# Window attention, MLP and dynamic convolution on one core: parameters folded inside the first rounds, softmax sums moved ahead, the taps' small network along the free axis

## The chip, the cores and the metric

The kernel runs on one core of a Trainium2 chip, in fp32. The metric is the device time of one execution in microseconds (us); lower is better. A core has five engines that work side by side (in the kernel before TensorE is busy for 95% of the span, VectorE for 66%, ScalarE for 51%, GpSimd for 21%), each on its own list of instructions: TensorE (matmul, "PE"), VectorE ("DVE"), ScalarE ("ACT"), GpSimd ("POOL") and SyncE ("SP", used here to issue DMA transfers). What stands in front of an instruction in that list can hold it up: below, copies stand behind a table load of 1.28 us and two convolution starts of 1.96 us together, and with these moved behind them (`a_tableys`) TensorE's 78.2 us of waits for copies are gone.

## The reference, cut to what matters

Layer 0 is a Swin block (window attention with shift, then an MLP), layer 1 a masked 3x3 depthwise convolution whose weights come from a small network on the pooled image.

```python
# x: (16, 192, 56, 56); 7x7 windows, 6 heads
h   = layernorm(x over channels) * g1 + b1            # rolled by -3, cut into windows
q, k, v = split(h @ qkv_w + qkv_b)                    # q scaled
p   = softmax(q @ k.T + rel_bias + mask)
x1  = x + unroll(p @ v @ proj_w + proj_b)
y   = x1 + gelu(layernorm(x1) * g2 + b2 @ fc1_w + fc1_b) @ fc2_w + fc2_b
t   = relu(batchnorm(mean(y over pixels) @ w1.T))     # 48 numbers per image
wt  = t @ w2.T + b2                                   # taps per channel and image, 4 of 9 used
out = depthwise_conv3x3(y, wt) + bias
```

## The kernel before

An image is cut into four strips, 64 in all; a strip is 7 rows of the upper half of the image and the 7 rows 28 below them. A **round** `i` does the MLP of strip `i-2` and the attention of strip `i` side by side, scales strip `i+1`, and takes statistics of strips `i+2` and `i-1`. The layer norms' gains and shifts are folded into the weights once, ahead of all rounds. The finished image is convolved in six **pieces**, one begun in the MLP's gap (`between`) and, when two more are ready, two begun on ScalarE ahead of the softmax copies.

```python
    images = {0: load_x(0, nc.sync)}          # the whole image, 1.48 MB
    # ... all parameters loaded (ScalarE's queue), folded on VectorE and TensorE ...

    def attention_scores(i, q4, q2):
        def add(wp):      # scores on TensorE, then e = scores + bias on VectorE
            ...
        def top(wp):      # maximum, subtraction (VectorE), Exp (ScalarE)
            ...
        def share(wp):    # sum, reciprocal (VectorE), product into prob (GpSimd)
            ...
        add(0)
        add(1)
        top(0)
        add(2)
        top(1)
        add(3)
        top(2)
        share(0)
        top(3)
        for wp in range(1, 4):
            share(wp)

    def attention_turn(i, wp):                # transposes of prob; two PSUM buffers
        pt = banks(f"pt_{i}_{wp}", wp % 2)
        ...                                   # six transposes
        prt = one.tile([128, 2, 3 * PW], F32, tag="prt", name=f"prt_{i}_{wp}", bufs=4)
        nc.scalar.copy(prt, pt[:, :, : 3 * PW])
        return prt

    def taps_second(b, tt):
        pw = bank(f"w_{b}", 1)
        for kc in range(2):
            for t in range(NTAP):
                c = kc * NTAP + t
                mm(pw[:, c : c + 1], w2t[:, kc, t, :], tt, True, True)
        ...

    for i in range(-2, NS + 2):
        keys = {}
        ...                                   # statistics (TensorE) of strips i+2 and i-1
        dev = norm_devs(keys) if keys else None       # square, Sqrt (ScalarE), reciprocal (VectorE)
        if has(i + 1):
            norm1_scale(i + 1, dvs.pop(0))
        if keys:
            dvs.update(norm_spread(keys, dev))        # deviation spread over partitions by DMA
        ...
            hid = one.tile([128, NFC, 2, T], F32, tag="hid", name=f"hid_{i - 2}")
            mlp_first(i - 2, yns.pop(i - 2), hid, between)
        ...
            table(AF.Exp)
            attention_scores(i, *qs.pop(i))
        table(AF.Sqrt)                        # loads the square root's table on ScalarE
        ys = [(*c, conv_begin(*c)) for c in conv_ready(2)]
        ...                                   # MLP second part on TensorE; a turn after each share of it
        o = attention_values(i, prts) if has(i) else None
        for c in ys:
            conv_rest(*c)
        if has(i + 1):
            qs[i + 1] = attention_qk(i + 1)
        ...                                   # taps_second, project, values of strip i+1
```

## Time and profile before

| | before |
|---|---|
| time, median of 3 executions | 3442.24 us (3442.2 to 3443.28) |
| TensorE busy | 3270.0 us, 95% |
| first scores / first MLP matmul | 98.95 / 190.45 us |
| steady cycle of four rounds (one image) | 205.44 us |

The lines that carry the bound are in the prediction. Where the texts say cold, TensorE ran at the slower pace of the start: a statistics matmul took 0.86 us at 58 us and 0.49 at 98. A row of a timeline gives the start, the duration from first to last, the engine, the source line, the operation with its tiles, the number of instructions joined in the row, and in brackets how long the engine had been idle and who ended that. Three more readings of the kernel before: the taps' matmuls (first rows), and the two deviations at the start. The second square (72.04) waits for the DMA that spreads the first deviation, as both use one tile.

```profile
61.13 0.49 ACT L382 ACTIVATE dev<-st 64x392 f32<-64x392 f32 x1 [20.51 <-PE st L89]
...
72.04 0.49 ACT L382 ACTIVATE dev<-st 64x392 f32<-64x392 f32 x1 [6.15 <-DMA dv<-dev]
...
1017.69 0.34 PE L89 MATMUL t<-pooled,w1t 128*48 128x1 f32 x4
...
1049.18 1.84 PE L89 MATMUL w<-tt,w2t 48*128 48x1 f32 x16
1050.95 1.41 PE L89 MATMUL pp<-o,wp 128*64 128x392 f32 x5
```

The groups of instructions give busy time and the mean in ns. The softmax's subtraction has a mean of 906 ns since the fourth of each round runs beside GpSimd's product (1.31 us at 1084.08, against 0.77 for each of the three before it).

```profile
L577 DVE TENSOR_TENSOR e<-e,top 113x588 f32<-113x588 f32 x256 | 231.9, 906 | 8.9
```

### The profile page before, as it was taken

How to read it: one execution, taken by the hardware profiler on the slowest of the kernel's cores; microseconds unless marked ns; L12 is line 12 of the kernel's file. 1: busy time of each engine (PE TensorE's matmuls, PEld its weight loads, DVE VectorE, ACT ScalarE, POOL GpSimd, SP SyncE). 2: the span in 40 equal slices, each digit the busy share in tenths (PEclk: the TensorE clock that was granted, in tenths of full speed). 3: DMA queues.
4: the chain of work that ended last, by engine and by line, in shares of the span. 5: the costliest groups of instructions: out<-in, count | busy, mean ns of one | idle time of the engine just before them, and what ended most of it. 6: DMA issues, size and time to landing. Idle time of an engine off the chain costs nothing.

```text
span 3441.8 us, 65409 instructions
## 1 busy us (share of the span) xinstructions
PE 3270.0 (95%) x26902; PEld 1937.9 (56%) x26902; DVE 2259.6 (66%) x4098; ACT 1765.9 (51%) x2884; POOL 734.6 (21%) x606
## 2 busy tenths in 40 slices
PE   4599999999999999999999999999999999999996
PEld 2455555556555555555555555555655555555553
DVE  2655576675766667576675866667576775857664
ACT  1454555555555555455555555555455555555553
POOL 1112212212212212212212212212221221221210
PEclk9799999999999999999999999999999999999998
DMA  2100111010110201111120110201112020111001
GB/s 68 43 20 11 48 39 48 25 56 25 42 54 25 62 24 35 47 39 50 31 62 13 46 48 28 58 24 39 44 38 55 26 62 18 40 48 33 26 19 53
DMA packets 83085, 135.34 MB, mean 39 GB/s; under 512 B 25537, under 2 KB 65890, under 8 KB 80738
## 3 DMA queue, kind: packets, MB, share of 16 engines
q1 hardware_dynamic: 76304, 128.65, 13.1%
q8 instruction: 212, 3.47, 0.4%
q10 hardware_dynamic: 6482, 2.51, 0.3%
q14 instruction: 87, 0.71, 0.1%
HBM read 41.15 MB, written 38.54 MB: 23 GB/s over the span
## 4 chain that ended last, share of the span: by engine, by line
PE 71%; DVE 18%; ACT 4%; issue 4%; POOL 1%; DMA 0%; ACTq 0%; SPq 0%; DVEq 0%; POOLq 0%
PE ph L89 24%; PE pv L89 8%; PE pp L89 7%; PE po L89 6%; DVE e L570 5%; PE st L89 5%; DVE top L576 5%; PE pk L89 4%; PE pf L89 4%; DVE e L577 4%; PE pq L89 4%; PE pe L89 4%; PE pt L607 3%; DVE tot L584 2%; ACT y L762 2%
## 5 line engine op out<-in xcount | busy, mean ns | idle before, releaser
L586 POOL TENSOR_TENSOR prob<-e,tot 113x588 f32<-113x588 f32 x256 | 295.3, 1175 | 2561.2 <-DVE tot L585 2561.2
L89 PE MATMUL ph<-yn,wf 128*128 128x392 f32 (+1 forms) x3072 | 819.2, 508 | 1.1 <-ACT hid L679 1.1
L89 PE MATMUL pf<-hid,wf 128*64 128x392 f32 (+1 forms) x3072 | 818.3, 497 | 0.0
L89 PEld LDWEIGHTS ph<-yn,wf 128*128 128x128 f32 (+1 forms) x3072 | 409.8, 187 | 401.8 <-ACT hid L679 85.0
L89 PEld LDWEIGHTS pf<-hid,wf 128*64 128x64 f32 (+1 forms) x3072 | 376.6, 163 | 310.7 <-issue 121.1
L679 ACT ACTIVATE hid<-ph,f1b 128x784 f32<-128x784 f32 x384 | 337.3, 914 | 216.6 <-PE ph L89 216.3
L477 DVE TENSOR_SCALAR kbd<-pk,qkb 32x784 f32<-32x784 f32 x256 | 263.7, 1030 | 281.0 <-PE pk L89 278.2
L580 ACT ACTIVATE e<-e 113x588 f32<-113x588 f32 x256 | 177.5, 693 | 420.6 <-DVE e L577 420.6
L777 DVE SCALAR_TENSOR_TENSOR y<-x,wt,y 128x770 f32<-128x770 f32 x288 | 342.6, 1199 | 23.8 <-ACT y L762 17.0
L570 DVE TENSOR_TENSOR e<-sc,bias_t 113x588 f32<-113x588 f32 x256 | 190.3, 764 | 226.5 <-PE sc L89 226.4
L89 PE MATMUL pv<-wqkv,win 64*128 64x192 f32 (+1 forms) x2048 | 275.8, 330 | 3.1 <-DVE kbd L477 3.1
L89 PEld LDWEIGHTS pv<-wqkv,win 64*128 64x128 f32 (+1 forms) x2048 | 253.7, 190 | 36.1 <-issue 18.3
L540 DVE COPY vbd<-pv 49x192 f32<-49x192 f32 x512 | 159.8, 350 | 173.0 <-PE pv L89 88.2
L607 PE MATMUL pt<-ident,prob 113*128 113x113 f32 x1536 | 199.0, 267 | 76.7 <-POOL prob L586 65.4
L607 PEld LDWEIGHTS pt<-ident,prob 113*128 113x128 f32 x1536 | 162.4, 143 | 190.6 <-POOL prob L586 159.1
L345 ACT ACT_TABLE_LOAD x199 | 255.3, 1283 | 3.5
L89 PE MATMUL pp<-o,wp 128*128 128x392 f32 (+2 forms) x896 | 250.7, 521 | 0.5 <-ACT o L639 0.5
L613 ACT COPY prt<-pt 128x678 f32<-128x678 f32 x256 | 180.9, 717 | 136.6 <-PE pt L607 136.5
L577 DVE TENSOR_TENSOR e<-e,top 113x588 f32<-113x588 f32 x256 | 231.9, 906 | 8.9
L724 DVE SCALAR_TENSOR_TENSOR x<-pf,f2b,x 128x784 f32<-128x784 f32 x64 | 66.2, 1034 | 230.6 <-PE pf L89 230.6
L542 ACT COPY vbd<-pv 49x192 f32<-49x192 f32 x512 | 135.4, 312 | 147.3 <-DVE vbd L540 147.3
L474 ACT ACTIVATE q<-pq,qkb 128x784 f32<-128x784 f32 x64 | 58.6, 916 | 290.3 <-PE pq L89 290.3
(114 smaller groups left out, 4236.6 us busy)
## 6 DMA issues: line engine op xcount, KB each, us to landing
dv<-dev SPq DMA_DIRECT2D x1024, 49.0 KB
x<-in_x_dram SPq DMA_DIRECT2D x16, 1484.0 KB
out_dram<-y SPq DMA_DIRECT2D x48, 392.0 KB
out_dram<-y SPq DMA_DIRECT2D x48, 196.0 KB
x<-in_x_dram SPq DMA_DIRECT2D x16, 392.0 KB
x<-in_x_dram SPq DMA_DIRECT2D x16, 350.0 KB
out_dram<-y SPq DMA_DIRECT2D x16, 308.0 KB
out_dram<-y SPq DMA_DIRECT2D x16, 154.0 KB
```

The costliest lines, as they stand in the source:

```text
L89: nc.tensor.matmul(dst, lhs, rhs, start=start, stop=stop, skip_group_check=True)
L345: nc.scalar.activation(junk, eps_t[0:1], func)
L477: nc.vector.tensor_scalar(kbd[p, 0:2, :, h % 2, :], pk[p, :, :T].rearrange("p h (w t) -> p h w t", t=N), qkb[p, 1:2], None, ALU.add,)
L570: nc.vector.tensor_tensor(e, sc[:PW, :, : HEADS * N], rel, ALU.add)
L576: nc.vector.tensor_reduce(t, ehs[wp], AX.X, ALU.max)
L577: nc.vector.tensor_tensor(ehs[wp], ehs[wp], t.broadcast_to([PW, 2 * HEADS, N]), ALU.subtract)
L580: nc.scalar.activation(es[wp], es[wp], AF.Exp)
L586: nc.gpsimd.tensor_tensor(prob[wp][:PW, :, 0:N], ehs[wp], t.broadcast_to([PW, 2 * HEADS, N]), ALU.mult)
L607: nc.tensor.transpose(pt[:, a, g * PW : (g + 1) * PW], prob[wp][:PW, h : h + 2, :].rearrange("p h k -> p (h k)"), ident[:PW, :PW],)
L613: nc.scalar.copy(prt, pt[:, :, : 3 * PW])
L679: nc.scalar.activation(hid[:, f], phs[f][:, :, :T], AF.Gelu, bias=f1b[:, f : f + 1])
L777: nc.vector.scalar_tensor_tensor(dst, src, wt[:, kc, t : t + 1], dst, ALU.mult, ALU.add)
```

## The change

Three parts. (1) Start: only what strip 0 needs is loaded first, strip by strip; the other parameters come on GpSimd's queue and are folded inside rounds 0 and 1, which get an order of their own. (2) Taps: the small network lies along the free axis, two matmuls and five VectorE instructions instead of 2 + 8 matmuls (each shows as two records in the trace: x4 and x16 above). (3) Softmax order: sums go ahead, so that GpSimd's product of one group no longer falls on the next subtraction and comes in time for the transposes. The diff, cut:

```diff
-        add(0)
-        add(1)
-        top(0)
-        add(2)
-        top(1)
-        add(3)
-        top(2)
-        share(0)
-        top(3)
-        for wp in range(1, 4):
-            share(wp)
+        if between is None:
+            add(0)
+            top(0)
+            add(1)
+            top(1)
+            share(0)
+            add(2)
+            top(2)
+            share(1)
+            add(3)
+            top(3)
+            share(2)
+        else:
+            ...                               # rounds 0 and 1: additions first
+        share(3)
...
-    def taps_first(b, pooled):
+    def taps(b, pooled):
         pt = bank(f"t_{b}", 1)
         for kc in range(2):
-            mm(pt[:RED, 0:1], w1t[:, kc, :], pooled[:, kc, :], kc == 0, kc == 1)
...
-                mm(pw[:, c : c + 1], w2t[:, kc, t, :], tt, True, True)
+            mm(pt[:, 0:RED], pooled[:, kc].broadcast_to([128, 128]), w1t[:, kc], kc == 0, kc == 1)
...
+    load_rows(*images[0], 0, 0, WS, nc.sync)              # strip 0: 7 rows of each half
+    nc.scalar.dma_start(raw[:, 0], qkv_w[0:C0])
...
+    load_rows(*images[0], 0, WS, 2 * WS, nc.sync)
+    load_rows(*images[0], 0, 2 * WS, HALF, nc.sync)
+    nc.sync.dma_start(mask_t, win_mask)
...                                                        # + 14 bias loads on the same queue
+    norm_squares("1_0", 0, 0, nc.gpsimd)
+    fold_scale(raw, g1, eff)
+    keys = stats_of(-2)
+    pm = fold_means(eff, 3 * DIM, "fq", 0)
+    dvs.update(norm_spread(keys, norm_devs(keys), (nc.sync, nc.scalar)))
+    norm_squares("1_1", 1, 0, nc.gpsimd)
+    fold_center(eff, 3 * DIM, pm)
...                                                        # wqkv, then the bias matmuls
+    keys = stats_of(-1)
+    dev = norm_devs(keys)
+    norm1_scale(0, dvs.pop(0), nc.vector)
...
+    for i, extra in ((0, (proj_bias, mlp_weights)), (1, (taps_weights,))):
+        attention_scores(
+            i, *qs.pop(i), lambda: norm1_scale(i + 1, dvs.pop(0), nc.gpsimd)
+        )
+        qs[i + 1] = attention_qk(i + 1)
+        for e in extra:
+            e()
+        keys = stats_of(i)
+        dev = norm_devs(keys)
...
```

## The prediction

> **What bounds the kernel now.** I read first the page's busy shares with its slices, then TensorE's waits from 200 to 3400 us, then the timelines of one steady round, and last those of the first 190 us.
>
> ```profile
> PE 3270.0 (95%) x26902; PEld 1937.9 (56%) x26902; DVE 2259.6 (66%) x4098; ACT 1765.9 (51%) x2884; POOL 734.6 (21%) x606
> ...
> PE   4599999999999999999999999999999999999996
> ...
> PEclk9799999999999999999999999999999999999998
> ```
>
> TensorE is full from the third slice to the last but one; only the first two slices (172 us) and the tail are thin. So in the middle a part matters only if it removes TensorE's work or one of its waits. TensorE's waits from 200 to 3400 us (total, times, longest) sum to 61.9 us, and nearly all are these two:
>
> ```profile
> PE pt L607 <- POOL prob L586: 47.5, 62, 0.8
> PE pt L607 <- ACT prt L613: 11.2, 29, 0.4
> ```
>
> 62 rounds wait 0.77 us once for GpSimd's softmax product. The second wait comes in the rounds in which ScalarE begins two convolution pieces ahead of its copies. One such round, TensorE, ScalarE and VectorE in turn:
>
> ```profile
> 1087.72 0.80 PE L607 MATMUL pt<-ident,prob 113*128 113x113 f32 x6 [0.77 <-POOL prob L586]
> 1088.36 1.50 PE L89 MATMUL pf<-hid,wf 128*128 128x392 f32 x4
> 1090.24 0.77 PE L607 MATMUL pt<-ident,prob 113*128 113x113 f32 x6 [0.39 <-ACT prt L613]
> ...
> 1085.42 0.69 ACT L580 ACTIVATE e<-e 113x588 f32<-113x588 f32 x1 [2.21 <-DVE e L577]
> 1086.13 1.28 ACT L345 ACT_TABLE_LOAD   x1
> ...
> 1087.54 1.96 ACT L762 ACTIVATE y<-x,cb,wt 128x784 f32<-128x784 f32 x2
> 1089.40 1.32 ACT L613 COPY prt<-pt 128x678 f32<-128x678 f32 x2
> ...
> 1084.08 1.31 DVE L577 TENSOR_TENSOR e<-e,top 113x588 f32<-113x588 f32 x1
> ```
>
> The second transpose (1087.72) waits for its probabilities; the third reuses the first one's PSUM bank and waits for its copy. That copy stands behind the fourth exponential, a table load and two convolution starts. The fourth exponential starts as VectorE's fourth subtraction ends, so that subtraction sets the third transpose.
>
> The start, TensorE's timeline:
>
> ```profile
> 79.25 2.98 PE L89 MATMUL pk<-win,wqkv 128*128 128x392 f32 x4 [14.14 <-DVE win L423]
> ...
> 98.95 1.23 PE L89 MATMUL sc<-kbd,q 64*64 64x98 f32 x48
> ...
> 145.41 1.74 PE L89 MATMUL sc<-kbd,q 64*64 64x98 f32 x72
> ...
> 190.45 4.75 PE L89 MATMUL ph<-yn,wf 128*128 128x392 f32 x14
> ```
>
> All weights are folded by 58 us; only then come the first statistics (58.2), the first projection (79), rounds 0 and 1 (about 45 us each), and the first MLP at 190.45. From there on TensorE is full.
>
> [...] a statistics matmul takes 0.86 us at 58 us and 0.49 at 98; but folding kept TensorE busy from 35 to 48 us without warming it. [...] 16 tap matmuls with 128-column weights advance 1.77 us, 111 ns each. [...] the fourth subtraction takes 1.31 us beside GpSimd's product, the others 0.77. [...] the 144 KB halves of the weights landed about 2.8 us after issue, and eight spreads of one deviation, issued in turn, took 6.5 us (65.5 to 72.0).
>
> **Part 1, the start.** I walk the new order with durations of the old trace.
> - Statistics of strip 0 need only its 600 KB, now loaded first. The first image's 1.48 MB transfer was in by 7.9 us, so the strip should be in by about 5.5. Squares on GpSimd 2.3, statistics (cold) until about 10, deviation chain as before (square 0.5, table load 1.28 which now lies on it, root 0.6, reciprocal 2.6) until about 15.
> - The spread goes half through the sync queue, behind 14 strips, the mask and 14 bias loads at about 0.6 us each, so it is issued at 17 to 20 and lands at 22 to 25. The second deviation reuses the tile, so it starts then: 5.1 us, then scaling; the first projection starts 2.8 us after the reciprocal, at about 31.
> - Projection to the end of the key copy 11.0 us, value part 9.8 (both from 79.25 to 100.05). The attention-bias sums (5.57 us) fit the 5.97 us in which VectorE waited there. First scores S0 at about 52 instead of 98.95.
> - Round 0 gets longer. VectorE: four additions, tops and shares to S0+13.3, keys to 17.5. Then the projection bias (about 3), first MLP weights scaled (0.5), their means on TensorE (about 4.5 cold), 24 bias matmuls (0.26 each cold as in 5.72 us for 22; here about 5), statistics 2, to about S0+33. Then deviation, transposes, values, projection and value part: second scores at S0+51. Before: 46.5.
> - Round 1: 9.6 us of softmax, keys 4.2; meanwhile eleven parameter loads on GpSimd's queue[...] land about 28 us in and stand before the deviation chain on ScalarE and VectorE. Reciprocal at 33.5, values and projection to 46, statistics 2.7: first MLP 49 us after the scores. Before: 45.0.
> - Sum: 52 + 51 + 49 = 152 instead of 190.45: **38.5 us gained**, about 47 by the early start less 8.5 given back.
>
> **Part 2, taps.** An image's taps cost TensorE 0.27 us (1017.69 to 1017.96) and 1.77 us (1049.18 to 1050.95) of advance. Now two matmuls, in four passes of 128 weight columns, about 0.5 us. 1.54 us by 15 images in the full stretch: **23 us gained**. VectorE gets five small instructions, about 1.5 us, in a gap of 5.5 us before the scores. The last image's taps shorten the tail by about 0.6.
>
> **Part 3, softmax order.** From the first addition, pitches are 0.69 for an addition (0.79 where its reduction follows directly), 1.48 for maximum and subtraction, 0.93 for sum and reciprocal. Old: the fourth subtraction ends after four additions, four tops with the slow subtraction, one share: 10.2 us, as seen. New: 4 x 0.79 + 4 x 1.48 + 2 x 0.93 = 10.9. The slow subtraction goes, but two shares and four bubbles stand before the end.
> - The second product is ready at 8.7 + 1.2 = 9.9 us, and TensorE comes at 11.7: the 0.77 us wait goes.
> - The fourth exponential starts 0.74 later, and so does the first copy. Third transpose without pieces: possible at 13.9, TensorE there at 13.7: wait 0.25. With pieces: possible at 15.0 + 0.74 = 15.7: wait 2.0 where both waits were 1.16.
> - 32 rounds gain 0.52, 30 lose 0.74 to 0.84: **about 6 us lost**.
>
> **Sum:** 3442.2 - 38.5 - 23 - 0.6 + 6 = 3386 us, 1.6% less.
>
> **Rivals.**
> - *The softmax order wins outright:* the 47.5 us go and nothing replaces them. For it: that wait is the largest. Against: ScalarE's copy already makes 29 waits of 0.39. If that did not move, 47 more would go: 3333.
> - *The start overlaps better:* the folding fills waits in which TensorE would idle anyway, and rounds 0 and 1 keep 45 us each: 47 gained, 3377. Against: bias matmuls stand before the statistics in TensorE's order, and the parameters before the deviation in VectorE's.
> - *GpSimd's queue becomes the bound of the start:* 16 loads before it scales strip 1, and 11 between its last product and the MLP input. [...] The page has no GpSimd load to size this by.
> - *The taps' saving is not real* since a broadcast operand loads slowly: 15 us less, 3401.
>
> **Range and chances.** Start 28 to 52 gained, taps 12 to 26, order from 12 lost to 25 gained: errors are independent, so some 30 us about the sum; 3352 to 3414. 2% less is about 3373, 13 below the middle: 0.29 faster, 0.70 same, 0.01 slower.
>
> **What would show it right or wrong.** The first scores at about 52 us and the first MLP matmul at about 152; waits of transposes for products gone, waits for copies grown to 50 to 70 us, about 2 us each with pieces; the tap matmuls down to four records of about 0.5 us an image; no slow fourth subtraction. I am wrong by most if the copy waits stay as they are, or if the first MLP stands far from 152.

## The result, and the profile after

| | before | after |
|---|---|---|
| time, median | 3442.22 us (3440.63 to 3443.28) | 3416.48 us (3415.19 to 3417.38) |
| ratio | | 0.9925, 95% interval 0.9908 to 0.9943 |
| first projection / first scores | 79.25 / 98.95 us | 41.22 / 61.86 us |
| second scores / first MLP matmul | 145.41 / 190.45 us | 119.79 / 172.73 us |
| cycle of four rounds | 205.44 us | 204.75 us |

The kernel before has one execution more here than in the first table. Here and below a ratio is the mean time of one kernel's fast executions over that of the other's in the same rounds, so not quite the ratio of the medians quoted. The gain is 0.75%, about 26 us where 56 were predicted, and the time lies 2.5 us above the range.

The page after: TensorE has 28.5 us less work and is as full as before.

```profile
PE 3241.5 (95%) x26642; PEld 1917.0 (56%) x26642; DVE 2256.0 (66%) x4143; ACT 1755.0 (51%) x2863; POOL 745.6 (22%) x656
...
PE   4799999999999999999999999999999999999996
...
PEclk8799999999999999999999999999999999999998
```

TensorE's waits from 200 to 3400 us (total us, times, longest): GpSimd's 47.5 us are gone and ScalarE's copies cost 78.2 us instead of 11.2.

```profile
PE pt L500 <- ACT prt L506: 78.2, 62, 2.6
```

The timeline after. In the round with two pieces ScalarE runs the table load (1065.37) and two convolution starts (1066.77) before its first copy, so the copies are late and the third transpose waits 2.22 us; in the next round, without pieces, 0.35 us.

```profile
41.22 2.98 PE L89 MATMUL pk<-win,wqkv 128*128 128x392 f32 x4 [7.95 <-DVE win L306]
...
61.86 3.54 PE L89 MATMUL sc<-kbd,q 64*64 64x98 f32 x96
...
119.79 0.73 PE L89 MATMUL sc<-kbd,q 64*64 64x98 f32 x24
...
172.73 12.78 PE L89 MATMUL ph<-yn,wf 128*128 128x392 f32 x48
...
1065.37 1.28 ACT L228 ACT_TABLE_LOAD   x1
...
1066.77 1.96 ACT L659 ACTIVATE y<-x,cols,wt 128x784 f32<-128x784 f32 x2
...
1068.64 1.31 ACT L506 COPY prt<-pt 128x678 f32<-128x678 f32 x2
1069.48 0.77 PE L500 MATMUL pt<-ident,prob 113*128 113x113 f32 x6 [2.22 <-ACT prt L506]
...
1119.63 0.77 PE L500 MATMUL pt<-ident,prob 113*128 113x113 f32 x6 [0.35 <-ACT prt L506]
```

Groups and one tile's view after: the subtraction is down to 779 ns, and the taps have four matmul records an image (64 in all) of 275 ns, which advance TensorE by 0.48 us (381.87 to 382.35).

```profile
L460 DVE TENSOR_TENSOR e<-e,top 113x588 f32<-113x588 f32 x256 | 199.4, 779 | 8.7
```

```profile
L89 PE MATMUL t<-w1t,pooled x64: 275/275/311, 381.9 to 3388.5; 128*128 128x48 f32 x64
```

The start after, all engines (SPq, ACTq and POOLq are issues on a queue). The squares of strip 0 start only at 13.74, put down to the mask's load; the 14 bias loads hold the sync queue from 13.63 to 26.43; so the sync half of the first spread goes out at 26.53, though its reciprocal ended at 23.23 and ScalarE's half went at 23.27. The second deviation starts only at 33.34, and what it waits for is not the spread but TensorE's statistics of strip 1, which begin at 30.43, behind the bias matmuls.

```profile
13.63 12.80 SPq L761 DMA_DIRECT2D rel_r<-in_L_conv_rel_bias_dram  x14
13.74 1.49 POOL L239 TENSOR_TENSOR sq<-x 128x784 f32<-128x784 f32 x1 [11.08 <-DMA mask_t<-in_win_mask_dram]
...
20.63 2.60 DVE L271 RECIPROCAL dev<-dev 64x392 f32<-64x392 f32 x1 [1.36 <-ACT dev L269]
...
23.27 2.52 ACTq L284 DMA_DIRECT2D dv<-dev  x4
...
26.53 15.55 SPq L284 DMA_DIRECT2D dv<-dev  x5
...
30.43 0.86 PE L89 MATMUL st<-x,sel 128*32 128x392 f32 x1
...
33.34 0.49 ACT L265 ACTIVATE dev<-st 64x392 f32<-64x392 f32 x1 [11.22 <-PE st L89]
...
81.25 0.67 PE L89 MATMUL bv_p<-cols,raw 128*64 128x1 f32 x4 [8.90 <-DVE cols L850]
...
85.08 6.35 PE L89 MATMUL ff_m<-wf,ones 128*128 128x384 f32 x8 [0.94 <-DVE wf L152]
91.36 6.23 PE L89 MATMUL f1b_p<-cols,raw 128*128 128x1 f32 x24
...
140.28 0.34 PE L878 MATMUL w1p<-ident,w1n 48*128 48x48 f32 x1 [9.19 <-DMA w1n<-in_L_conv_w_dram]
```

The last four rows lie in rounds 0 and 1: TensorE waits 8.90 us for the projection bias, spends 12.6 us on the MLP's means and biases, and waits 9.19 us for a taps parameter whose load GpSimd issued at 138.22, behind its last product.

### The profile page after: what moved, and what is told of

It reads as the page before. It is cut to its first block, busy times and chain, and to the rows that moved or that the text cites.

```text
span 3415.0 us, 65067 instructions
## 1 busy us (share of the span) xinstructions
PE 3241.5 (95%) x26642; PEld 1917.0 (56%) x26642; DVE 2256.0 (66%) x4143; ACT 1755.0 (51%) x2863; POOL 745.6 (22%) x656
## 4 chain that ended last, share of the span: by engine, by line
PE 68%; DVE 20%; ACT 7%; issue 3%; DMA 1%; POOL 0%; SPq 0%; DVEq 0%; ACTq 0%; POOLq 0%
PE ph L89 24%; PE pv L89 7%; PE pp L89 7%; DVE top L459 6%; DVE e L453 5%; PE po L89 5%; PE st L89 5%; DVE e L460 5%; PE pk L89 4%; PE pq L89 4%; PE pe L89 4%; PE pf L89 3%; DVE tot L467 3%; PE pt L500 3%; ACT L228 2%
## 5 line engine op out<-in xcount | busy, mean ns | idle before, releaser
L674 DVE SCALAR_TENSOR_TENSOR y<-x,wt,y 128x770 f32<-128x770 f32 x288 | 322.9, 1131 | 22.7 <-ACT y L659 15.9
L617 DVE SCALAR_TENSOR_TENSOR x<-pf,cols,x 128x784 f32<-128x784 f32 x64 | 66.2, 1035 | 246.5 <-PE pf L89 246.5
L271 DVE RECIPROCAL dev<-dev 128x392 f32<-128x392 f32 (+1 forms) x67 | 174.4, 2602 | 48.7 <-ACT dev L269 48.7
L460 DVE TENSOR_TENSOR e<-e,top 113x588 f32<-113x588 f32 x256 | 199.4, 779 | 8.7
```

The costliest lines, as they stand in the source:

```text
L460: nc.vector.tensor_tensor(ehs[wp], ehs[wp], t.broadcast_to([PW, 2 * HEADS, N]), ALU.subtract)
L674: nc.vector.scalar_tensor_tensor(dst, src, wt[:, kc, t : t + 1], dst, ALU.mult, ALU.add)
```

## The experiments

My theory after the result: the taps are right; the start lost 21 us of its predicted gain to waits in series that the walk had not seen; the softmax order costs about 13 us, not 6, since everything ScalarE has in front of its copies now falls on TensorE. Rivals: the order is harmless and the start explains all; or TensorE's clock differs. All runs below are correct in their results.

### One part at a time: the old order back, the new order alone, the taps alone

`a_oldorder` is the changed kernel with the old list of `add`, `top` and `share`; `b_neworder` and `b_taps` are the kernel before with one part of the change.

```diff
 # a_oldorder, on the kernel after
-            add(0)
-            top(0)
-            add(1)
-            top(1)
-            share(0)
...
+            add(0)
+            add(1)
+            top(0)
+            add(2)
+            top(1)
...
 # b_neworder: the reverse, on the kernel before
 # b_taps, on the kernel before
-    def taps_first(b, pooled):
-    def taps_second(b, tt):
+    def taps(b, pooled):                      # as in the change, with its parameters
```

> The changed kernel with the softmax order of before put back in the full rounds. Theory 1 (the new order costs time: the copies' waits that it creates outweigh the products' waits that it removes, about 15 us by subtraction of the other parts in the trace): about 3401 us, with 62 waits of 0.77 us of transposes for products back and copy waits down to 29 of 0.39. Rival (the new order is a gain, and the missing gain is lost in the start alone): 3416 to 3450.

> The kernel before with the new softmax order alone. Theory 1: slower by about 15 us, 3457 us, and TensorE's waits of transposes go from 59 us to about 78, all for copies. Rival: faster by up to 47 us, since the largest wait of TensorE goes.

> The kernel before with the new taps' network alone. Theory 1: 1.56 us less of TensorE per image in 15 full rounds and 0.5 in the tail: about 3418 us. Rival (broadcast weight loads are slow, and the gain of the whole change came from elsewhere): 3430 to 3442.

| run | time | ratio to before |
|---|---|---|
| a_oldorder | 3404.4 us (3402.69 to 3406.51) | 0.9893 [0.9878, 0.9908] |
| b_neworder | 3475.83 us (3474.42 to 3476.05) | 1.0099 [1.0082, 1.0116] |
| b_taps | 3418.09 us (3416.97 to 3418.54) | 0.9932 [0.9917, 0.9947] |

The **taps** are worth 24.1 us (3442.2 - 3418.1), near the predicted 23 + 0.6. So the rival of slow broadcast loads (3430 to 3442) is out. The match is partly luck: in the profiled executions the first MLP matmul of `b_taps` already comes 4.5 us earlier (185.99 against 190.45), and from there to the last scores it is 21.6 us faster (3119.6 against 3141.2). The **order** costs 12.1 us between the changed kernel and `a_oldorder` by the medians, and 12.7 in the profiled executions from the first MLP matmul to the end (172.73 to 3415.0 against 175.11 to 3404.7). The waits of `a_oldorder` are those of before:

```profile
PE pt L500 <- POOL prob L469: 47.7, 62, 1.0
PE pt L500 <- ACT prt L506: 11.6, 30, 0.4
```

`b_neworder` lost 33.6 us, 19 more than expected. Its waits are as expected, all for copies (76.2 us in 62), so the further 19 us are not waits. Its timeline and a stretch of 5 us (the third last figure of the row is the granted clock) show where the time went: right behind a 2.22 us wait four matmuls take 2.84 us instead of 1.50, at a granted clock of 0.77 over the stretch.

```profile
473.58 1.11 PE L608 MATMUL pt<-ident,prob 113*128 113x113 f32 x6 [2.22 <-ACT prt L614]
474.48 2.84 PE L89 MATMUL pf<-hid,wf 128*128 128x392 f32 x4
```

```profile
475.00:480.00 5.00, 5.00 (x82) 3.64 (x82) 2.60 (x4) 1.17 (x2) 3.29 (x3) 0.77 0.01 3
```

I took all 5 us stretches from 200 to 3250 us and summed what the clock withheld (the expectations below call such a dip a half-clock window). `b_neworder` has 12 such dips of 1.7 us each, 20.4 us; the kernels before and after, `a_oldorder` and `b_taps` have none there. Beyond 3250 us `b_neworder` has a 13th (3378.6 us) and the changed kernel one (3269.7 us). Without the dips the order costs 33.6 - 22.1 = 11.5 us here and 12.7 - 1.7 = 11.0 there. So the same order, with the same 2.22 us waits, costs a further 20 us in one kernel and nearly nothing in the other, which differs in its start and its taps.

### ScalarE's path to the copies cleared

`a_tableys` keeps the new order but moves the table load behind the copies of the outputs and the two convolution starts behind turns 1 and 2. `a_table` and `a_ys` do one each; `a_old_tableys` puts the old order on `a_tableys`.

```diff
-        table(AF.Sqrt)
-        ys = [(*c, conv_begin(*c)) for c in conv_ready(2)]
+        ready = conv_ready(2)
+        ys = []
...
                 prts.append(attention_turn(i, wp))
+            if wp in (1, 2) and ready:
+                c = ready.pop(0)
+                ys.append((*c, conv_begin(*c)))
...
         o = attention_values(i, prts) if has(i) else None
+        table(AF.Sqrt)
```

> The changed kernel with two things of ScalarE put behind the copies: the load of the root's table goes behind the output copies, and the two convolution starts go behind the second and third copy. Theory 1 (the copies wait only for what stands before them on ScalarE): copies 1.5 us earlier in each round and another 1.9 in rounds with pieces, transposes wait for nothing, about 78 us less: 3338 to 3345 us. Rival (some other wait takes its place, for instance VectorE's key copies behind the later convolution pieces): above 3370.

> The changed kernel with only the square-root table load moved behind the copies of the outputs. Theory (the wait is the sum of what stands in front of the first copy on ScalarE: a 1.28 us table load in every round, two 0.96 us starts in 30 of 62): waits of 0.35 vanish and those of 2.2 become 0.9, so 27 us are left of 78; total 3360 to 3370. Rival (VectorE's later fourth subtraction sets it, not ScalarE's queue): waits stay above 60 us.

> The changed kernel with only the two convolution starts moved behind turns 1 and 2. Theory: all rounds now wait 0.35 us, 62 times, 20 to 24 us in all, and the starts give a little back elsewhere; total 3355 to 3366. Rival as for the other part: waits stay above 60 us.

> The version without the late copies (table load behind the copies of the outputs, the two convolution starts behind turns 1 and 2; 3351.8 us) with the old softmax order put back. Theory (the new order is right once ScalarE's path is clear, and lost here only by what stood in front of the copies): TensorE's waits for GpSimd's product come back, about 47 us in 62 waits, those for copies stay away, total 3386 to 3396. Rival (it was the copies alone, the order is worth nothing): total within 8 us of 3352.

| run | time | ratio to before | TensorE's waits for copies |
|---|---|---|---|
| after | 3416.48 us | 0.9925 | 78.2 us in 62 |
| a_table | 3360.0 us (3359.74 to 3361.42) | 0.9762 [0.9746, 0.9778] | 21.6 us in 30 |
| a_ys | 3371.81 us (3371.0 to 3372.8) | 0.9795 [0.9781, 0.981] | 22.3 us in 62 |
| a_tableys | 3351.79 us (3350.52 to 3353.02) | 0.974 [0.9725, 0.9754] | none |
| a_old_tableys | 3400.37 us (3398.3 to 3400.95) | 0.9877 [0.9861, 0.9894] | none |

The waits are additive in ScalarE's queue as expected: without the table load the rounds without pieces wait no more and the others about 0.7 us; without the starts all 62 rounds wait about 0.36 us. `a_ys` is 6 us slower than its range though its waits are as expected; 2.4 us are new waits for VectorE's key copies, 1.5 us lie before its first MLP matmul (174.19 against 172.73), the rest I did not find. Both together take all waits for copies away, but the time is 7 us above its range, as some 15 us come back at the value matmuls, which now wait for VectorE's key copies behind two pieces' taps (waits of `a_tableys`):

```profile
PE pv L89 <- DVE kbd L360: 14.8, 28, 0.7
```

`a_old_tableys` answers the question of the order. With the path cleared, the old order waits for GpSimd's product again (its time is 4 us above its range):

```profile
PE pt L500 <- POOL prob L469: 47.0, 61, 1.1
```

So clearing ScalarE's path is worth 4 us under the old order (3404.4 to 3400.4) and 65 us under the new (3416.5 to 3351.8), and the new order costs 12 us with the path blocked and gains 49 us with it clear. The order moved the bound from GpSimd to ScalarE's queue: alone it costs time, and clearing the path alone pays little.

### The start: early squares, early spread

The squares of strip 0 read 7 rows of each half in one access, which spans the rows of the other strips that lie between them. The profile put their wait down to the mask's load, the last one to end; whether it was that or the strips' loads, these runs tell. `a_split` takes one instruction per half. `a_rel` issues the mask and the 14 bias loads behind the first spread. `a_splitrel` does both.

```diff
 # a_split
-            engine.tensor_tensor(s0, v0, v0, ALU.mult)
+            if key in ("1_0", "1_1"):
+                for h in range(2):
+                    engine.tensor_tensor(s0[:, h], v0[:, h], v0[:, h], ALU.mult)
+            else:
+                engine.tensor_tensor(s0, v0, v0, ALU.mult)
 # a_rel
-    nc.sync.dma_start(mask_t, win_mask)       # and the 14 loads of rel_r
...
     dvs.update(norm_spread(keys, norm_devs(keys), (nc.sync, nc.scalar)))
+    nc.sync.dma_start(mask_t, win_mask)       # and the 14 loads of rel_r
```

> The changed kernel with the squares of strips 0 and 1 taken in two instructions, one per row half, so that an access no longer spans the rows of strips 2 and 3 that lie between. Theory 1 (the squares of strip 0 waited for loads they do not need, and the sync queue, on which 14 bias loads stand before half of the spread, is a second bound of its own): squares start at about 6 to 8 us instead of 13.7, but the first projection (41.2) and first scores (61.9) move by under 3 us, and the total by under 3 us. Rival (the squares alone held the start): first projection at about 34, first MLP matmul at about 166 instead of 172.7, total about 3410.

> The changed kernel with the mask and the 14 bias loads issued behind the spread of the first deviation on the sync queue. Theory 1: the spread goes out as its reciprocal ends, at about 23.3 instead of 26.5, so the first projection comes about 3 us earlier (38), first scores at about 59; total about 3413, unless the bias sums now wait for their loads. Rival (the loads had no part, for the second deviation or GpSimd sets the projection): nothing moves.

> Both edits. Theory 1: squares at 6 to 8 us, spread out at about 17, first projection at about 31 to 33 as the prediction had it, first scores at 52 to 54, and the gain is more than the sum of the two single edits; first MLP matmul at 163 to 166, total 3406 to 3410. Rival (rounds 0 and 1 fill up again what the start gains, since they wait for parameters from GpSimd's queue): first scores at 52 to 54 but first MLP matmul still near 172, total near 3416. A further rival: TensorE's half-clock windows come back with another phase of the rounds, and the total rises while the first MLP matmul is earlier.

| run | first projection | first scores | first MLP matmul | time | clock dips in the profiled execution, 200 to 3250 us |
|---|---|---|---|---|---|
| after | 41.22 | 61.86 | 172.73 | 3416.48 us (3415.19 to 3417.38) | 0 |
| a_split | 37.16 | 58.59 | 167.88 | 3432.94 us (3424.32 to 3438.0) | 12 |
| a_rel | 40.64 | 62.87 | 172.87 | 3441.96 us (3417.74 to 3444.34) | 16 |
| a_splitrel | 36.88 | 58.45 | 170.65 | 3439.74 us (3421.69 to 3442.7) | 4 |

Two findings. First, **the start**: the squares did start at 5.2 instead of 13.7, and with both edits the spread went out at 18.80 instead of 26.53, and still the first projection came only 4 us earlier, nearly all of it by the squares alone (`a_split`: 4.1 us, where under 3 were expected, and about 7 by the rival). `a_splitrel` was expected at 31 to 33. Its timeline names two more waits behind these: the statistics of strip 1 stand behind the bias matmuls on TensorE (26.09), and the scaling of strip 0 stands behind the second deviation on VectorE, though the first one's spread was issued by 21.6.

```profile
18.80 2.50 SPq L288 DMA_DIRECT2D dv<-dev  x4
...
25.48 0.67 PE L89 MATMUL qkb_p<-cols,raw 128*64 128x1 f32 x4 [0.24 <-DVE qkb L803]
26.09 0.86 PE L89 MATMUL st<-x,sel 128*32 128x392 f32 x1
...
29.00 0.49 ACT L269 ACTIVATE dev<-st 64x392 f32<-64x392 f32 x1 [11.34 <-PE st L89]
...
36.88 2.98 PE L89 MATMUL pk<-win,wqkv 128*128 128x392 f32 x4 [7.95 <-DVE win L310]
```

`a_rel` alone moved the first projection by 0.6 us, nearly nothing, as its rival had it: the spread went out 3.9 us earlier, but the second deviation still waited for TensorE's statistics (32.76 instead of 33.34). And it names the first wait: with the mask gone from the queue the squares start at 13.15 all the same, now put down to the loads of the image's rows.

```profile
13.15 1.49 POOL L239 TENSOR_TENSOR sq<-x 128x784 f32<-128x784 f32 x1 [10.49 <-DMA x<-in_x_dram]
...
22.67 2.49 SPq L284 DMA_DIRECT2D dv<-dev  x4
...
32.76 0.49 ACT L265 ACTIVATE dev<-st 64x392 f32<-64x392 f32 x1 [11.23 <-PE st L89]
```

Second, **the clock**: earlier starts made slower kernels. The time lost to dips explains it: the profiled spans less the dips (1.7 us each) are 3409.7 for `a_split`, 3414.8 for `a_rel` and 3413.1 for `a_splitrel`, against 3415.0 for the changed kernel, which follows the first MLP matmuls (5 us, 0 and 2 us earlier; kernels whose start is the same have it at 172.73 to 175.57, so 3 us are scatter). And executions of one kernel now differ: `a_rel` took 3443.8, 3440.2, 3444.3 and 3417.7 us. The timeline of `a_split` and its stretch show the same pattern as `b_neworder`:

```profile
450.35 0.77 PE L504 MATMUL pt<-ident,prob 113*128 113x113 f32 x6 [2.22 <-ACT prt L510]
450.96 2.49 PE L89 MATMUL pf<-hid,wf 128*128 128x392 f32 x4
```

```profile
450.00:455.00 5.00, 4.65 (x30) 3.20 (x31) 1.51 (x3) 1.93 (x4) 4.85 (x5) 0.66 0.01 3
```

### Is it the 2 us waits that bring the dips?

`c_split_ys` has the early squares of `a_split` and the starts of the pieces moved as in `a_ys`, so that no steady round has a wait over 0.7 us.

```diff
 # a_split, and
-        ys = [(*c, conv_begin(*c)) for c in conv_ready(2)]
+        ready = conv_ready(2)                 # begun behind turns 1 and 2, as in a_ys
```

> The early squares that brought 13 half-clock windows (profiled 3430 us, 22 us lost to them), with the two convolution starts moved as well, so that no wait of 2.2 us is left in the rounds. Theory [...]: no half-clock windows between 200 and 3250 us, total 3 to 6 us under the run with the starts moved alone, spread between executions under 4 us. Rival (the early start itself shifts the load so that the clock drops): about 13 windows remain and the total is 15 us or more above that.

Measured: 3369.53 us (3365.68 to 3370.14), ratio 0.9785 [0.9769, 0.9802]; no dip between 200 and 3250 us instead of 12; 2.3 us under `a_ys`, which is what its earlier first MLP matmul gives (171.94 against 174.19), and less than the 3 to 6 expected. The spread is 4.5 us, a little over the 4 expected. In all runs dips between 200 and 3250 us came only in kernels with 2.2 us waits. So taking the 2 us waits away took the dips away, at nearly the same early start.

Why the same waits gave 0, 4, 12 and 16 dips was not shown. Each of the 44 dips withheld 1.70 to 1.75 us, but not every wait of 2.22 us is followed by one. Around and behind that of `b_neworder` which ends at 473.58, the granted clock is 0.89 and 0.77 (first figure after the length: TensorE's busy time)

```profile
470.00:475.00 5.00, 2.78 (x12) 1.75 (x11) 1.00 (x4) 4.32 (x7) 4.93 (x5) 0.89 0.00 0
475.00:480.00 5.00, 5.00 (x82) 3.64 (x82) 2.60 (x4) 1.17 (x2) 3.29 (x3) 0.77 0.01 3
```

and at that of the changed kernel which ends at 1069.48 it is 1.00 throughout, with TensorE busy for the same 2.78 of 5 us:

```profile
1065.00:1070.00 5.00, 2.78 (x18) 1.72 (x16) 1.86 (x6) 4.92 (x7) 4.27 (x4) 1.00 0.00 0
1070.00:1075.00 5.00, 5.00 (x109) 4.23 (x107) 3.34 (x4) 1.45 (x2) 4.83 (x4) 1.00 0.00 0
```

The changed kernel, `a_split`, `a_rel` and `a_splitrel` have nearly the same waits for copies (60 to 62, 75.8 to 78.2 us in all) and differ in the start. That the start sets the number of dips, as it moves all later waits together, is inference. There is one profile of each kernel; that the executions of one kernel differ for the same reason is inferred too, not shown.

### A base without those waits, and the start and the rounds on it

To read the start without these dips, `s_base` puts one piece in the MLP's gap and one behind it, in three of four rounds, on `a_tableys`. `s_start` adds the two edits of the start and two more: strip 1's statistics ahead of the bias matmuls (these in one go), and the scaling ahead of the second deviation. `s_fold` adds to `s_base` a new order of rounds 0 and 1. `s_all` has both.

```diff
 # s_base
-        ready = conv_ready(2)
+        ready = conv_ready(1)                 # and the taps ahead of the piece in between()
 # s_start, with a_split and a_rel
     norm_squares("1_1", 1, 0, nc.gpsimd)
+    keys = stats_of(-1)
     fold_center(eff, 3 * DIM, pm)
...
-    keys = stats_of(-1)
-    dev = norm_devs(keys)
     norm1_scale(0, dvs.pop(0), nc.vector)
+    dev = norm_devs(keys)
 # s_fold, rounds 0 and 1
-        for e in extra:
-            e()
+        if i == 1:
+            mlp_weights()                     # means and biases of the MLP
         keys = stats_of(i)
         dev = norm_devs(keys)
...
+        if i == 0:
+            proj_bias()                       # behind the turns
+            fold_scale(rawf, g2, wf1)
...                                           # taps' parameters loaded before round 0
```

> On top of the run in which the table load and the two convolution starts left ScalarE's way: one convolution piece now in TensorE's MLP stretch and one behind it, in three of four rounds, and the taps ahead of the piece. That run had 28 waits of the value matmuls for VectorE's key copies, 14.8 us. If those come from two pieces in one round: they go, total about 3337 (3330 to 3342). Rival (the pieces only move the wait to another place): total 3348 to 3355, with a new wait of TensorE of 10 us or more.

> On top of the last version (one convolution piece in the MLP stretch, no late copies; TensorE's half-clock windows do not occur there): squares per half, bias loads behind the spread, and in addition the statistics of strip 1 ahead of the bias matmuls on TensorE and the scaling of strip 0 ahead of the second deviation on VectorE. The two runs with the first two edits showed the first projection at 37 where the spread had gone out 4.5 us earlier, since the second deviation waited for those bias matmuls. Theory (four waits in series held the start, each found only when the one before it was gone): first projection at 27 to 30 instead of 40.6, first scores at 48 to 51 instead of 62.8, first MLP matmul at 160 to 163 instead of 173, total 3330 to 3333 instead of 3342.5. Rival (rounds 0 and 1 wait for their parameters on GpSimd's queue and give it back): first scores as early, first MLP matmul at 168 or later, total 3338 or more.

> On top of the last version, the start untouched, but rounds 0 and 1 with the folding out of the way: strip 2's statistics ahead of it on TensorE, the projection bias and the MLP weights' scaling behind the deviation, the 24 bias matmuls and the means in round 1, the taps' parameters loaded early. Theory (folding in front of statistics and deviation made rounds 0 and 1 57.9 and 52.9 us long): first scores unchanged at 62.8, first MLP matmul at 148 to 155 instead of 173, total 3318 to 3325. Rival (the rounds are long since TensorE is cold[...], whatever the order): first MLP matmul at 166 or later.

> Both together. If the start and the rounds are two separate terms, their gains add: first MLP matmul at 135 to 143, total 3305 to 3313. If they hide each other: no better than the better of the two by more than 4 us.

| run | first projection | first scores | second scores | first MLP matmul | time | ratio to before |
|---|---|---|---|---|---|---|
| s_base | 40.63 | 62.84 | 121.51 | 172.97 | 3342.48 us | 0.9711 [0.9697, 0.9726] |
| s_start | 28.48 | 50.76 | 109.43 | 161.29 | 3332.15 us | 0.968 [0.9665, 0.9694] |
| s_fold | 41.40 | 63.02 | 107.22 | 160.91 | 3330.22 us | 0.9675 [0.966, 0.9689] |
| s_all | 29.54 | 51.20 | 95.40 | 149.10 | 3319.56 us | 0.9643 [0.9628, 0.9657] |

`s_base` lies half a microsecond above its range (3330 to 3342); the 14.8 us at the value matmuls are gone, and 10.7 us of 15 short waits of the scores for VectorE came instead. `s_start` hit all its numbers: with the four waits removed (how much each of the last three is worth by itself was not isolated) the first projection comes at 28.5, and the 12.1 us gained there reach the first MLP matmul (11.7) and the time (10.3). So the first rounds do not swallow an earlier start; the rival is out. `s_fold` made round 0 14.5 us shorter (44.2 instead of 58.7) but round 1 2.2 us longer (53.7), as the folding had only moved there: 12.3 us instead of 18 to 24. The two gains add up: 10.3 + 12.3 = 22.6, and `s_all` gains 22.9 us, though its own numbers were 7 us lower (3305 to 3313).

### Round 1, and the best version

In `s_all` TensorE's statistics in round 1 wait for VectorE's MLP bias. `s_best` moves the 24 bias matmuls into TensorE's wait in round 0 and the means of round 1 behind its second turn.

```diff
-        if i == 1:
-            mlp_weights()
         keys = stats_of(i)
+        pf = mlp_bias() if i == 0 else None
...
-        prts = [attention_turn(i, wp) for wp in range(4)]
+        prts = [attention_turn(i, wp) for wp in range(2)]
+        if i == 1:
+            mlp_weights()                     # the means alone
+        prts += [attention_turn(i, wp) for wp in range(2, 4)]
```

> The version with start and folding mended (3319.6 us, first MLP matmul at 149.1, round 1 53.7 us long), with the 24 MLP bias matmuls in round 0 behind strip 2's statistics, and round 1's MLP means behind its second turn instead of ahead of its statistics. Theory (round 1 is long since its statistics wait for VectorE's centring and the bias matmuls): round 1 46 to 49 us, first MLP matmul at 142 to 145, total 3312 to 3316. Rival (the bias matmuls only move the delay into round 0): first scores of round 1 3 us or more later, total 3318 or more.

Measured: 3310.9 us (3310.07 to 3312.33), ratio 0.9619 [0.9604, 0.9633], 3.1% under the changed kernel's median. Its start, in TensorE's timeline:

```profile
28.64 2.98 PE L89 MATMUL pk<-win,wqkv 128*128 128x392 f32 x4 [3.68 <-DVE win L310]
...
50.45 3.72 PE L89 MATMUL sc<-kbd,q 64*64 64x98 f32 x96
...
94.64 0.73 PE L89 MATMUL sc<-kbd,q 64*64 64x98 f32 x24
...
137.91 12.78 PE L89 MATMUL ph<-yn,wf 128*128 128x392 f32 x48
```

Round 1 is 43.3 us long instead of 53.7, and round 0 as long as in `s_all`. This is better than expected (46 to 49): round 1's length was the folding that stood before its statistics.

## Why the prediction was wrong

**The total.** It came out 30 us above the predicted middle. About 21 us of that is the start (17.7 gained instead of 38.5), 6 to 7 us the order, 1 to 2 us the taps in the full rounds. The profiled executions close the sum: 17.7 us less to the first MLP matmul (190.45 to 172.73), 9.5 less from there to the last scores (3141.2 to 3131.8: 21.6 by the taps less 12.1 for the order) and 0.4 more behind them give 26.8 us (3441.8 - 3415.0).

**Part 1, "statistics of strip 0 need only its 600 KB".** This step failed first. The squares ran at 13.74, not at 5.5, as their access reaches over the rows of later strips, whose loads they had to wait for (`a_rel` names them); `a_split` alone moved them to 5.2. The reciprocal ended at 23.2 instead of 15.

**Part 1, "the second deviation reuses the tile, so it starts then" (22 to 25), "first projection ... at about 31".** Here the mechanism failed: the step took the spread for the last wait before the second deviation. The queue was named as a cause, but with the wrong size: the bias loads took 0.91 us each (12.80 us for 14) instead of 0.6, so its half went out at 26.53. `a_rel` shows that this was not the last wait: with the spread out at 22.67 the second deviation came at 32.76 instead of 33.34. It waited for the statistics of strip 1, which stood behind bias matmuls on TensorE, and the scaling stood behind it. From there the walk was right: 7.9 us from the second deviation to the projection at 41.22, as predicted (5.1 + 2.8). With all four waits gone (`s_start`) the projection is at 28.5. From the projection to the scores the prediction was right (21 us predicted, 20.6 measured).

**Part 1, "second scores at S0+51".** Measured S0+57.9. Statistics 2 ended at S0+38.4 instead of S0+33: the projection bias resumed about 2 us late, the means took 6.35 us instead of 4.5, the 24 bias matmuls 6.23 instead of 5, all at half clock; and a 2.56 us wait for a copy was not in the walk. The two sizes could have been read from the kernel before, where eight records of the means took 1.62 + 4.78 us and 22 bias matmuls 5.72. `s_fold` shows that this length was the folding's place: 44.2. The stretches of the kernel after, for the means and for the biases (granted clock third from the end):

```profile
85.00:92.00 7.00, 6.92 (x11) 2.63 (x11) 1.00 (x2) 0.00 (x0) 0.00 (x0) 0.50 0.00 0
92.00:98.00 6.00, 6.00 (x26) 5.55 (x30) 1.45 (x3) 0.00 (x0) 0.00 (x0) 0.50 0.00 0
```

TensorE is busy for 12.92 of these 13 us at a granted clock of 0.50. This agrees with the prediction's remark on the kernel before: TensorE was busy there for 12.58 us of the 13 from 35 to 48, and the folding's records have the same pace (0.80 and 0.26 us each) from the first to the last. The view of granted clocks must not be trusted there: it gives 1.00 up to 65.49 us, where the trace's clock records begin, even over the statistics at 58 us, which take 0.86 us instead of 0.49.

**Part 1, "values and projection to 46, statistics 2.7: first MLP 49 us after the scores".** Values and projection did end at 46.0 us after the second scores (165.76 - 119.79). What the step left out is the value part of strip 2, 4.27 us, which stands between. With it the sum is 46.0 + 4.3 + 2.7 = 53.0, as measured (52.9). The parameters on GpSimd's queue took 0.52 to 0.59 us each to issue, and though TensorE stood 9.19 us for the first of them, values and projection ended where the walk had them: the third rival, GpSimd's queue as the bound of the start, did not come true.

**Part 2.** Right: 1.77 + 0.27 became 0.48 us per image, 24.1 us in all with the tail and the earlier start of `b_taps`; 21.6 in the full rounds, where 23 were predicted.

**Part 3.** The mechanism was right: GpSimd's wait gone, copies' waits in its place, 0.35 and 2.2 us where 0.25 and 2.0 were predicted, no slow subtraction. The size was off: "about 6 us lost" was 12 to 13. Rounds without pieces gained 0.44 us (50.58 to 50.14) instead of 0.52 and rounds with pieces lost 0.83 (51.17 to 52.0): 30 x 0.83 - 32 x 0.44 = 10.8 us, where the prediction's own figures give 30 x 0.79 - 32 x 0.52 = 7.1, written as 6. A further 1.7 us is the dip at 3269.7. The first rival (the order wins outright) was ruled out for this kernel, but it is what happens once ScalarE's path is clear.

**The range.** Start and order both came out at or beyond the bad end of their own ranges (start 17.7 of "28 to 52", order 12 to 13 lost of "12 lost to 25 gained"), and the errors added up. Whether they were independent, as the range assumed, two terms can't show; the start's own range was too narrow.

## What to carry to other kernels

When a wait is removed, list what stands in front of the next wait on every engine, and move that too: the new order cost 12 us alone and gained 49 with ScalarE's queue cleared. Walk a start through each engine's own order and each access's true extent, not through the data that a step needs; here four waits stood in series, and removing the first gave 4 us, all four 12. And look at the granted clock behind waits of 2 us: here such a wait could cost 1.7 us on top of its own 2.22, at some starts (12 times in `a_split`) and not at others (never between 200 and 3250 us in the changed kernel). Where the trace has no clock records yet, compare the pace of like matmuls.
